# A four-layer graph network on one core: window sums carried by TensorE, VectorE's side work placed behind the messages, operands moved to PSUM

## The chip, the cores and the metric

The kernel runs on one core of a Trainium2 chip. The time is the device time of one execution in microseconds (us); before the change the median of three runs is 5459.54 us (5449.31 to 5473.62). The core has five engines with queues of their own, each in order: TensorE (PE in the profile; its weight loads are PEld), VectorE (DVE), ScalarE (ACT), GpSimd (POOL) and SyncE (SP). Here GpSimd does nothing but issue indirect DMAs, which gather or scatter one row of memory for each of 128 partitions, and SyncE issues the plain DMAs.

## The reference

Four layers update 6250 nodes of 160 numbers (64 scalars and 32 vectors of 3) over 100000 edges that are sorted by their target `dst`. Each layer does this, with its own weights and small differences:

```python
h = relu(layernorm(x))                    # nodes
f = h @ W_lin                             # node rows, "table" in the kernel
w = act(edge_features @ W_fc1) @ W_fc2    # weights of every edge
m = tensor_product(f[src], edge_attr, w)  # 384 numbers an edge (480 in layer 2)
agg = segment_sum(m, dst, N)
x = x + mix(agg @ W_out, h @ W_skip)
```

Layers 0, 1 and 3 gather by `src` and sum by `dst`. Layer 2 takes rows by `dst` and sums by `src`, by which the edges are not sorted.

## The kernel before

Edges are cut into 784 tiles of 128, and 14 tiles (`WT`) make a window; there are 56 windows. The edges of a window hit fewer than 128 nodes, since they are sorted. The tiles of a window's two halves alternate, and each half's targets fit in 64 nodes. Two windows make a unit `u`, and four tiles make a group `g`, so a layer has 196 groups. There is a second program for irregular inputs, which isn't taken here.

`edges(li)` (L1205 on) does layers 0, 1 and 3. For each group:

- `gather` (L1277): four indirect DMAs on GpSimd bring the rows `f[src]` of 128 edges each into `ge`. It is called six groups ahead, and there are eight `ge` buffers.
- `hidden` (L1266 or L1260, L1269) and `edge_weights` (L1300 or L1293, L1304, L1306): TensorE computes the edge weights, ScalarE brings them out of PSUM, partly scaled by an edge number, to `ws`.
- `messages` (L1313 to L1338): seven VectorE instructions. `oh` (L1319) is a one-hot of each edge's target among 64 nodes, from `iota` and the targets' places `loc`, both in SBUF. `pr`, `dot` and four parts of `msg` are products of `ge`, `ws` and edge numbers. The edge numbers were copied (L1313) for each unit into a PSUM tile, `yls`.
- TensorE adds `oh` times `msg` to `pg` in PSUM (L1394), 64 rows a half window. At a window's end ScalarE copies `pg` to `acc` (L1397).

Then `nodes` works on a window's 128 rows of `acc` as a Python generator, two steps of it a group. `turn` (L1346) is a matrix that puts the rows of both halves in order. In `nodes_out` four matmuls by `turn` make `pt_out` (L1062), ScalarE copies it to `at` (L1069), TensorE makes `po` (L1080, L1082), and VectorE adds to the node rows (L1095, L1096 and on). Then `nodes_in` makes the next layer's table: norm (L991 to L888), `hn` (L999), transposes (L1009, L1010), `pa` (L1022), `tb` (L1031 or L1033), and a DMA to memory. The next layer's first gather waits for all of it. A target on the border of two windows has part of its sum in each. Column 0 of `at` is the part that a window hands on, and VectorE adds it to column 1 of the next window's `at` (L1073).

In layers 0 and 1 another generator, `positions` (`self.sort`), sorts the edges by `src` for layer 2. For each of 53 buckets of 120 nodes and one more, VectorE makes `hit` (L1166), a running sum over 784 columns (the scan, L1168, from bfloat16 `hit` and `zeros_b` in SBUF), and two products or sums of 784 columns (L1171, L1172). One step is taken every third group.

Layer 2 has two stages. In `messages2` TensorE selects target rows out of `tb` (the window's 128 table rows) by a one-hot `oh` that VectorE makes of the window's targets (L1447: 1792 columns, from `dt`, a broadcast of the targets' numbers, L1445). `pe` (L1479) holds the selected rows, `pw` (L1468) the edge weights, VectorE makes `row` (L1497 to L1506), and GpSimd scatters each edge's 390 numbers to its sorted place (L1509). There are five `row` buffers. `sums2` then reads them back in order (L1601 to L1624) with plain DMAs.

The order of each engine's instructions is set when the program is built: a scheduler places the instructions of all these generators by its own estimate of times and priorities, so that node steps and sort steps stand between the messages of a group where it thinks they fit.

Of the kernel before, what the change touches and what calls it, by code (L numbers as in the profile page):

```python
# [689 lines left out]
class Fast:  # L690
# [16 lines left out]
    def prologue(self):  # L707
# [343 lines left out]
    def nodes_out(self, li, xt, sk, acc, turn, carry, w, wk, pp):  # L1051
# [5 lines left out]
        for k in range(4):  # L1057
            rows, o = (96, 3 * MV) if k == 0 else (MV, (k - 1) * MV)
            if turn is None:
                nc.tensor.transpose(pt[:rows, k, :], acc[:, o : o + rows], self.ident[:n, :n])  # L1060
            else:
                nc.tensor.matmul(pt[:rows, k, :], lhsT=acc[:, o : o + rows], rhs=turn, start=True, stop=True)  # L1062
        yield
# [4 lines left out]
        else:  # L1068
            nc.scalar.copy(at, pt)  # L1069
        if turn is not None:  # L1070

            if carry[0] is not None:
                nc.vector.tensor_add(at[:, :, 1], at[:, :, 1], carry[0][:, :, 0])  # L1073
            carry[0] = at
        yield
# [66 lines left out]
    def positions(self, wk):  # L1142
# [21 lines left out]
        for b in range(BK + 1):  # L1164
            hit = wk.tile([P, TT], BF16, name="hit2", bufs=2)
            nc.vector.tensor_scalar(hit, self.src_b, float(b), None, op0=ALU.is_equal)  # L1166
            cum = wk.tile([P, TT], F32, name="cum", bufs=2)
            nc.vector.tensor_tensor_scan(cum, hit, self.zeros_b, self.off[:, b : b + 1], op0=ALU.add,  # L1168
                                         op1=ALU.add)
# [29 lines left out]

    def at(self, k, most=N):  # L1200

        return self.nc.values_load(self.first[0:1, 2 * k : 2 * k + 1], engines=[mybir.EngineType.SP], min_val=0, max_val=most,
                                   skip_runtime_bounds_check_because="a node's number")

    def edges(self, li):  # L1205
# [19 lines left out]

        yls = p_y.tile([P, 2, 3, 2 * WT], F32, name="yls")

# [81 lines left out]
        def messages(u, g):  # L1309
            n = width(u, g)  # L1310
            rt, yl = data[u][0], yls[:, u % 2]
            if g == 0:
                nc.vector.tensor_copy(yl, rt[:, :, 1:4].rearrange("p t c -> p c t"))  # L1313
            ws = wss.pop((u, g))[:, :n]
            ge = gath.pop((u, g))[:, :n]
            gs = slice(G * g, G * g + n)
            oh = wk.tile([P, G, HN], F32, name="oh", bufs=3)
            t0 = 2 * WT * u + G * g
# [6 lines left out]
            yv = yl[:, :, gs].rearrange("p c t -> p t c")  # L1325
            t1 = msg[:, :, AW : AW + 64]
# [10 lines left out]
            tt(mvec[:, :, :, 0:64], by3(t1, 64), yv[:, :, :, None].to_broadcast([P, n, 3, 64]), ALU.mult)  # L1337
            tt(mvec[:, :, :, 64:96], e1, by3(ws[:, :, 64:96], 32), ALU.mult)  # L1338
            return oh, msg

        carry = [None]

        def nodes(k, acc):
            xt, sk = xts.pop(k)
            turn = nk.tile([P, P], F32, name="turn")
# [36 lines left out]
        for i, (u, g) in enumerate(groups):  # L1382
            prepare(i + AHEAD)
            weights_of(i + 2)
            if i + 1 < len(groups):
                edge_weights(*groups[i + 1])
            oh, msg = messages(u, g)
            for k in range(width(u, g)):
# [6 lines left out]
                if end:  # L1395
                    acc = wk.tile([P, AW], F32, name="acc")
# [14 lines left out]
    def messages2(self):  # L1411
# [26 lines left out]
        def select(k):  # L1438

            n = min(WT, TT - WT * k) * P  # L1440
            at = self.at(k)
            tb = ld.tile([P, 160], F32, name="tb")
            nc.sync.dma_start(tb, self.table[2][ds(at, P), :])
# [3 lines left out]
            nc.vector.tensor_scalar(oh.rearrange("p t e -> p (t e)")[:, :n], dt[:, :n], self.plus_w[:, k : k + 1], None,  # L1447
                                    op0=ALU.is_equal)
            ohs[k] = tb, oh
# [22 lines left out]
        def messages(u, g):  # L1472
            n = width(u, g)
            t0 = 2 * WT * u + G * g
            ts = slice(t0, t0 + n)
            pe = p_e.tile([P, G, 256], F32, name="pe")
            for k in range(n):
                tb, oh = ohs[(t0 + k) // WT]
                nc.tensor.matmul(pe[:, k, :160], lhsT=oh[:, (t0 + k) % WT, :], rhs=tb, start=True, stop=True)  # L1479
            pw = pws.pop((u, g))[:, :n]  # L1480
            pe = pe[:, :n]
            row = wk.tile([P, G, RW], F32, name="row", bufs=5)[:, :n]
            ev = wk.tile([P, G, 224], F32, name="ev", bufs=3)[:, :n]
            nc.scalar.copy(ev[:, :, 0:160], pe[:, :, 0:160])
            nc.scalar.copy(ev[:, :, 160:224], pe[:, :, 64:128])
            nc.scalar.copy(row[:, :, 294:390], pe[:, :, 64:160])  # L1486
            nc.scalar.copy(row[:, :, 256:262], self.edge_in[:, ts, :])
# [165 lines left out]
def _layout(inputs):  # L1653
# [46 lines left out]
    a["dst_t"] = by_tile(i["dst"], 1 << 20).T  # L1700
    a["dst_w"] = by_tile(i["dst"], 1 << 20).reshape(NW, WT * P)
    rec0 = np.zeros((E, 8), np.float32)
# [58 lines left out]
```

## Time and profile before

| what | value |
|---|---|
| median of runs | 5459.54 us |
| profiled execution, and its span | 5448.67, 5446.9 us |
| busy: PE, DVE, POOL, ACT | 4624, 4218, 3346, 2087 us |
| granted TensorE clock, mean | 0.881 |
| prologue up to the first gather | 171.4 us |
| layer 0, first to last gather | 171.4 to 1265.3 |
| layer 1, first to last gather | 1323.7 to 2394.8 |
| layer 2, first to last scatter | 2454.7 to 3549.9 |
| layer 2, sums | 3549.9 to 4379.9 |
| layer 3, first to last gather | 4379.9 to 5419.7 |
| one gather, min / median / max | 941 / 946 / 4311 ns |

A line of the groups' part reads: source line, engine, operation, tile written <- tiles read, how many; then busy us and mean ns of one; then the engine's idle time just before them and what ended it. In an order of time the columns are start, duration, engine, line. Busy time of TensorE is latency: matmuls overlap each other, so it is not occupancy.

### The profile page before, as it was taken

The page shows a single profiled execution, that of the slowest core. Times are in us where ns is not written, and L with a number is a line of the kernel's source. Part 1 is how long each engine was busy: PE and PEld are TensorE (multiplying, and loading weights), DVE is VectorE, ACT ScalarE, POOL GpSimd, SP SyncE. Part 2 cuts the span into 40 slices and gives each one's busy share as a digit, 9 for nine tenths or more (in the row PEclk, how much of TensorE's full clock was granted, in tenths as well). Part 3 has the DMA queues.
Part 4 walks back from the last instruction along what each step waited for, and adds up shares of the span by engine and source line. Part 5 has one row for each costly group of instructions (what it writes and reads, how often), then busy time and mean ns, then how long its engine had stood idle before and what let it go on. Part 6 is the DMA issues. An engine that isn't in the chain of part 4 may idle for free.

```text
span 5446.9 us, 77043 instructions
## 1 busy us (share of the span) xinstructions
PE 4624.0 (85%) x22084; PEld 2866.7 (53%) x22084; DVE 4217.8 (77%) x11655; ACT 2087.1 (38%) x6858; POOL 3346.0 (61%) x3143
## 2 busy tenths in 40 slices
PE   6799999997999999976666666689999988888887
PEld 4455555554555555544444444478888844444443
DVE  6688889888878897867777777767777767777777
ACT  5344444443544444533333333312222243343433
POOL 0577777774777777747777777700000067777776
PEclk9899999998989898987787877799999978788887
DMA  3333333322333333336666666477777533333332
GB/s 95 105 97 88 91 87 90 88 75 73 98 94 94 90 95 93 90 101 239 215 219 215 222 218 223 166 283 237 238 235 237 164 87 80 82 81 82 83 79 57
DMA packets 371211, 733.89 MB, mean 135 GB/s; under 512 B 69677, under 2 KB 249098, under 8 KB 370650
## 3 DMA queue, kind: packets, MB, share of 16 engines
q1 hardware_dynamic: 207122, 379.11, 22.3%
q0 software_dynamic: 163072, 349.43, 22.0%
q8 instruction: 180, 2.95, 0.2%
q14 instruction: 253, 2.07, 0.1%
q10 hardware_dynamic: 584, 0.33, 0.0%
HBM read 519.59 MB, written 209.08 MB: 134 GB/s over the span
## 4 chain that ended last, share of the span: by engine, by line
PE 52%; DVE 16%; DMA 14%; POOL 6%; issue 5%; ACT 3%; SPq 0%; DVEq 0%; ACTq 0%; POOLq 0%
PE pg L1394 12%; PE pg L1613 7%; DMA rec<-row,edge_to 7%; PE pw L1300 7%; DMA ge<-table,rt 6%; PE pg L1611 5%; POOL ge L1277 5%; PE ph L1266 4%; PE pa L1022 3%; PE pt_out L1062 2%; PE po L1082 2%; POOL rec L1509 2%; PE ph L1455 2%; DVE msg L1337 2%; PE pw L1293 2%
## 5 line engine op out<-in xcount | busy, mean ns | idle before, releaser
L1277 POOL DMA_INDIRECT ge<-table,rt x2352 | 2489.1, 1058 | 1774.1 <-DMA skip<-sk 830.3
L1394 PE MATMUL pg<-msg,oh 128*64 128x384 f32 x4704 | 1061.4, 572 | 165.6 <-DVE msg L1338 139.7
L1509 POOL DMA_INDIRECT rec<-row,edge_to x784 | 856.1, 1092 | 299.0 <-issue 191.2
L1304 ACT ACTIVATE ws<-pw,rt 128x96 f32<-128x96 f32 x2352 | 695.8, 348 | 820.5 <-DVE msg L1338 298.6
L1300 PE MATMUL pw<-w_w2y,hh 100*128 100x192 f32 x3136 | 673.5, 353 | 10.6 <-ACT ws L1306 7.7
L1394 PEld LDWEIGHTS pg<-msg,oh 128*64 128x64 f32 x4704 | 305.9, 150 | 709.0 <-issue 252.5
L1300 PEld LDWEIGHTS pw<-w_w2y,hh 100*128 100x128 f32 x3136 | 534.9, 202 | 236.9 <-ACT ws L1306 138.6
L1337 DVE TENSOR_TENSOR msg<-msg,yls 128x768 f32<-128x768 f32 x588 | 555.7, 945 | 0.0
L1613 PE MATMUL pg<-msg,oh 128*120 128x288 f32 x1668 | 541.5, 406 | 0.0
L1330 DVE TENSOR_TENSOR pr<-ge,yls 128x384 f32<-128x384 f32 x588 | 320.2, 545 | 220.7 <-DMA ge<-table,rt 219.9
L1269 ACT ACTIVATE hh<-ph 100x1024 f32<-100x1024 f32 (+1 forms) x336 | 269.1, 801 | 463.7 <-PE pw L1293 206.2
L1479 PE MATMUL pe<-tb,oh 128*128 128x160 f32 x1568 | 348.4, 363 | 112.5 <-ACT row L1486 112.3
L1266 PE MATMUL ph<-ft,w_w1r 12*100 12x512 f32 (+1 forms) x784 | 382.3, 658 | 71.2 <-ACT hh L1269 57.0
L1611 PE MATMUL pg<-rt,oh 128*120 128x192 f32 x1668 | 410.0, 328 | 29.3 <-DMA rt<-rec 29.3
L1479 PEld LDWEIGHTS pe<-tb,oh 128*128 128x128 f32 x1568 | 277.6, 226 | 274.5 <-ACT row L1486 221.9
L1333 DVE TENSOR_TENSOR msg<-ws,ge 128x512 f32<-128x512 f32 x588 | 402.0, 684 | 0.0
L1306 ACT COPY ws<-pw 128x192 f32<-128x192 f32 x1176 | 388.5, 330 | 0.0
L1455 PE MATMUL ph<-ft,w_w1d 128*128 128x512 f32 x224 | 162.4, 819 | 263.2 <-ACT hh L1457 262.4
L1502 DVE TENSOR_TENSOR row<-pw,ev 128x512 f32<-128x512 f32 x196 | 135.2, 690 | 301.8 <-ACT row L1488 298.3
L1611 PEld LDWEIGHTS pg<-rt,oh 128*120 128x120 f32 x1668 | 298.0, 184 | 117.6 <-issue 30.7
L1331 DVE TENSOR_REDUCE dot<-pr 128x128 f32<-128x384 f32 x588 | 344.2, 585 | 0.1
L1338 DVE TENSOR_TENSOR msg<-ge,ws 128x384 f32<-128x384 f32 x588 | 324.4, 552 | 0.0
(486 smaller groups left out, 7327.6 us busy)
## 6 DMA issues: line engine op xcount, KB each, us to landing
rt<-rec SPq DMA_DIRECT2D x208, 780.0 KB
dt<-in_dst_w_dram SPq DMA_DIRECT2D x56, 896.0 KB
ge<-table,rt POOLq DMA_INDIRECT x2352
ft<-in_ft_dram SPq DMA_DIRECT2D x56, 512.0 KB
ft<-in_ft_dram SPq DMA_DIRECT2D x28, 896.0 KB
xt<-x SPq DMA_DIRECT2D x168, 82.0 KB
rec<-row,edge_to POOLq DMA_INDIRECT x784
rt<-in_rec_dram SPq DMA_DIRECT2D x84, 112.0 KB
```

What stands on the lines that cost most here:

```text
L1266: nc.tensor.matmul(ph[:, i], lhsT=w1[r : r + K, :], rhs=ft[r : r + K, 4 * P * (j // 2) :][:, : 4 * P], start=True, stop=True)
L1277: nc.gpsimd.indirect_dma_start(out=ge[:, k, :], out_offset=None, in_=self.table[li], in_offset=bass.IndirectOffsetOnAxis(ap=rt[:, G * g + ...
L1300: nc.tensor.matmul(pw[:, i, :192], lhsT=hh[:, k + i, :], rhs=w2, start=True, stop=True)
L1304: nc.scalar.activation(ws[:, k0 + i, 0:96], pw[:, i, 0:96], AF.Copy, scale=rt[:, G * g + k0 + i, 0:1])
L1306: nc.scalar.copy(ws[:, k0 : k0 + m, 96:192], pw[:, :m, 96:192])
L1333: tt(msg[:, :, AW - 64 : AW + 64].rearrange("p g (k u) -> p g k u", k=2), ws.rearrange("p g (k u) -> p g k u", k=2)[:, :, :, 0:64], e0[:, ...
L1337: tt(mvec[:, :, :, 0:64], by3(t1, 64), yv[:, :, :, None].to_broadcast([P, n, 3, 64]), ALU.mult)
L1394: nc.tensor.matmul(pg[half], lhsT=oh[:, k, :], rhs=msg[:, k, :AW], start=t % WT < 2, stop=t % WT >= WT - 2)
L1479: nc.tensor.matmul(pe[:, k, :160], lhsT=oh[:, (t0 + k) % WT, :], rhs=tb, start=True, stop=True)
L1509: d = nc.gpsimd.indirect_dma_start(out=self.rec2, out_offset=bass.IndirectOffsetOnAxis(ap=self.edge_to[:, t0 + k : t0 + k + 1], axis=0), i ...
L1611: nc.tensor.matmul(pg[:, 0:192], lhsT=oh[:, k, :], rhs=rt[:, k, 0:192], start=first, stop=end, skip_group_check=True)
L1613: nc.tensor.matmul(pg[:, 192:480], lhsT=oh[:, k, :], rhs=msg[:, k, :], start=False, stop=end, skip_group_check=True)
```

## The change

- **Carried sums.** VectorE's addition of the handed-on column (L1073) is gone. In its place, after each of the four matmuls of `pt_out`, a matmul of one column adds the previous window's `acc` times column 0 of its `turn` onto column 1 of `pt_out`. `acc` and `turn` have four buffers each.
- **Node steps and sorting.** The steps of `nodes` and of `self.sort` that a group takes are built under `tc.issue_after(last.ins)`: their VectorE instructions may not stand before the group's last message instruction.
- **Operands in PSUM.** `yls` becomes part of a tile `bank`, which also holds the targets' places of a unit (copied from `loc`) and one zero. `oh` reads the targets there, and the scan reads the zero there, as float32.
- **Row groups in layer 2.** The 64 target nodes of a half window take one half of the partitions: `tb` and `dt` are loaded by halves, `oh` has half as many columns, and the matmuls of `pe` take 64 rows each, alternating between the two row halves and writing to two PSUM banks. `plus_w` is made from `column` to suit.

```diff
@@ prologue
-        nc.vector.tensor_scalar(self.plus_w, pw[:, 0, :], iota_p, None, op0=ALU.add)
         column = pro.tile([P, NW], F32, name="column0")
         nc.vector.tensor_scalar(column, pw[:, 1, :], place, None, op0=ALU.add)
+        nc.vector.scalar_tensor_tensor(self.plus_w, column, -1.0, pw[:, 0, :], op0=ALU.add, op1=ALU.add)
@@ nodes_out
-            else:
-                nc.tensor.matmul(pt[:rows, k, :], lhsT=acc[:, o : o + rows], rhs=turn, start=True, stop=True)
+                continue
+            nc.tensor.matmul(pt[:rows, k, :], lhsT=acc[:, o : o + rows], rhs=turn, start=True, stop=carry[0] is None,
+                             skip_group_check=True)
+            if carry[0] is not None:
+                sums, turned = carry[0]
+                nc.tensor.matmul(pt[:rows, k, 1:2], lhsT=sums[:, o : o + rows], rhs=turned[:, 0:1], start=False,
+                                 stop=True, skip_group_check=True)
+        if turn is not None:
+            carry[0] = acc, turn
...
-        if turn is not None:
-            if carry[0] is not None:
-                nc.vector.tensor_add(at[:, :, 1], at[:, :, 1], carry[0][:, :, 0])
-            carry[0] = at
@@ positions
-            nc.vector.tensor_tensor_scan(cum, hit, self.zeros_b, self.off[:, b : b + 1], op0=ALU.add,
+            nc.vector.tensor_tensor_scan(cum, hit, self.zero.to_broadcast([P, TT]), self.off[:, b : b + 1], op0=ALU.add,
                                          op1=ALU.add)
@@ edges
-        yls = p_y.tile([P, 2, 3, 2 * WT], F32, name="yls")
+        bank = p_y.tile([P, 8 * 2 * WT + 1], F32, name="bank")
+        yls = bank[:, : 8 * 2 * WT].rearrange("p (u c t) -> p u c t", u=2, c=4)
+        self.zero = bank[:, 8 * 2 * WT :]
+        nc.vector.memset(self.zero, 0.0)
...
-                nc.vector.tensor_copy(yl, rt[:, :, 1:4].rearrange("p t c -> p c t"))
+                nc.vector.tensor_copy(yl[:, 0:3], rt[:, :, 1:4].rearrange("p t c -> p c t"))
+                nc.vector.tensor_copy(yl[:, 3], self.loc[:, 2 * WT * u : 2 * WT * u + 2 * WT])
...
             tt(oh[:, :n], self.iota[:, None, :HN].to_broadcast([P, n, HN]),
-               self.loc[:, t0 : t0 + n, None].to_broadcast([P, n, HN]), ALU.is_equal)
+               yl[:, 3, gs, None].to_broadcast([P, n, HN]), ALU.is_equal)
...
-            tt(mvec[:, :, :, 64:96], e1, by3(ws[:, :, 64:96], 32), ALU.mult)
-            return oh, msg
+            last = tt(mvec[:, :, :, 64:96], e1, by3(ws[:, :, 64:96], 32), ALU.mult)
+            return oh, msg, last
...
-            live = [n for n in live if not (next(n, True) or next(n, True))]
+            with tc.issue_after(last.ins):
+                live = [n for n in live if not (next(n, True) or next(n, True))]
             if li < 2 and i % 3 == 0:
-                next(self.sort, None)
+                with tc.issue_after(last.ins):
+                    next(self.sort, None)
@@ messages2
-            dt = ld.tile([P, WT * P], I32, name="dt", bufs=2)
-            nc.sync.dma_start(dt[:, :n], self.a["dst_w"][k : k + 1, :n].to_broadcast([P, n]))
-            oh = ld.tile([P, WT, P], F32, name="oh", bufs=3)
+            dt = ld.tile([P, WT // 2 * P], I32, name="dt", bufs=2)
+            for h in range(2):
+                rows = slice(HN * h, HN * h + HN)
+                nc.sync.dma_start(tb[rows], self.table[2][ds(self.at(k, half=h), HN), :])
+                nc.sync.dma_start(dt[rows], self.a["dst_w"][2 * k + h : 2 * k + h + 1, :].to_broadcast([HN, WT // 2 * P]))
+            oh = ld.tile([P, WT // 2, P], F32, name="oh", bufs=3)
...
-                nc.tensor.matmul(pe[:, k, :160], lhsT=oh[:, (t0 + k) % WT, :], rhs=tb, start=True, stop=True)
+                h, rows = k % 2, slice(HN * (k % 2), HN * (k % 2) + HN)
+                nc.tensor.matmul(pe[:, 2 * h + k // 2, :160], lhsT=oh[rows, (t0 + k) % WT // 2, :], rhs=tb[rows],
+                                 start=True, stop=True)
```

More of the change, by code (lines that the diff above doesn't have):

```diff
@@ L1198, in layers, with at @@
         es.close()
-    def at(self, k, most=N):
-        return self.nc.values_load(self.first[0:1, 2 * k : 2 * k + 1], engines=[mybir.EngineType.SP], min_val=0, max_val=most,
+    def at(self, k, most=N, half=0):
+        return self.nc.values_load(self.first[0:1, 2 * k + half : 2 * k + half + 1], engines=[mybir.EngineType.SP], min_val=0, max_val=most,
                                    skip_runtime_bounds_check_because="a node's number")
@@ L1317, in messages @@
             oh = wk.tile([P, G, HN], F32, name="oh", bufs=3)
-            t0 = 2 * WT * u + G * g
             tt(oh[:, :n], self.iota[:, None, :HN].to_broadcast([P, n, HN]),
-               self.loc[:, t0 : t0 + n, None].to_broadcast([P, n, HN]), ALU.is_equal)
+               yl[:, 3, gs, None].to_broadcast([P, n, HN]), ALU.is_equal)
             msg = wk.tile([P, G, AW + 64], F32, name="msg", bufs=3)[:, :n]
@@ L1324, in messages @@
             e1 = ge[:, :, 64:160].rearrange("p g (c u) -> p g c u", c=3)
-            yv = yl[:, :, gs].rearrange("p c t -> p t c")
+            yv = yl[:, 0:3, gs].rearrange("p c t -> p t c")
             t1 = msg[:, :, AW : AW + 64]
@@ L1344, in nodes @@
             xt, sk = xts.pop(k)
-            turn = nk.tile([P, P], F32, name="turn")
+            turn = nk.tile([P, P], F32, name="turn", bufs=4)
             nc.vector.tensor_scalar(turn, self.iota, self.column[:, k : k + 1], None, op0=ALU.is_equal)
@@ L1386, in edges @@
                 edge_weights(*groups[i + 1])
-            oh, msg = messages(u, g)
+            oh, msg, last = messages(u, g)
             for k in range(width(u, g)):
@@ L1395, in edges @@
                 if end:
-                    acc = wk.tile([P, AW], F32, name="acc")
+                    acc = wk.tile([P, AW], F32, name="acc", bufs=4)
                     nc.scalar.copy(acc, pg)
@@ L1438, in select @@
         def select(k):
-            n = min(WT, TT - WT * k) * P
-            at = self.at(k)
             tb = ld.tile([P, 160], F32, name="tb")
-            nc.sync.dma_start(tb, self.table[2][ds(at, P), :])
-            dt = ld.tile([P, WT * P], I32, name="dt", bufs=2)
-            nc.sync.dma_start(dt[:, :n], self.a["dst_w"][k : k + 1, :n].to_broadcast([P, n]))
-            oh = ld.tile([P, WT, P], F32, name="oh", bufs=3)
-            nc.vector.tensor_scalar(oh.rearrange("p t e -> p (t e)")[:, :n], dt[:, :n], self.plus_w[:, k : k + 1], None,
+            dt = ld.tile([P, WT // 2 * P], I32, name="dt", bufs=2)
[4 more added lines that the diff above has]
+            oh = ld.tile([P, WT // 2, P], F32, name="oh", bufs=3)
+            nc.vector.tensor_scalar(oh.rearrange("p t e -> p (t e)"), dt, self.plus_w[:, k : k + 1], None,
                                     op0=ALU.is_equal)
@@ L1478, in messages @@
                 tb, oh = ohs[(t0 + k) // WT]
-                nc.tensor.matmul(pe[:, k, :160], lhsT=oh[:, (t0 + k) % WT, :], rhs=tb, start=True, stop=True)
+                h, rows = k % 2, slice(HN * (k % 2), HN * (k % 2) + HN)
+                nc.tensor.matmul(pe[:, 2 * h + k // 2, :160], lhsT=oh[rows, (t0 + k) % WT // 2, :], rhs=tb[rows],
+                                 start=True, stop=True)
+            pe = pe.rearrange("p (h t) c -> p t h c", h=2)
+            pair = lambda v: v.rearrange("p (t h) c -> p t h c", h=2)
             pw = pws.pop((u, g))[:, :n]
-            pe = pe[:, :n]
             row = wk.tile([P, G, RW], F32, name="row", bufs=5)[:, :n]
             ev = wk.tile([P, G, 224], F32, name="ev", bufs=3)[:, :n]
-            nc.scalar.copy(ev[:, :, 0:160], pe[:, :, 0:160])
-            nc.scalar.copy(ev[:, :, 160:224], pe[:, :, 64:128])
-            nc.scalar.copy(row[:, :, 294:390], pe[:, :, 64:160])
+            nc.scalar.copy(pair(ev[:, :, 0:160]), pe[:, :, :, 0:160])
+            nc.scalar.copy(pair(ev[:, :, 160:224]), pe[:, :, :, 64:128])
+            nc.scalar.copy(pair(row[:, :, 294:390]), pe[:, :, :, 64:160])
             nc.scalar.copy(row[:, :, 256:262], self.edge_in[:, ts, :])
@@ L1700, in _layout @@
     a["dst_t"] = by_tile(i["dst"], 1 << 20).T
-    a["dst_w"] = by_tile(i["dst"], 1 << 20).reshape(NW, WT * P)
+    a["dst_w"] = np.append(i["dst"], np.full(TT * P - E, 1 << 20, np.int32)).reshape(2 * NW, WT // 2 * P)
     rec0 = np.zeros((E, 8), np.float32)
```

## The prediction

> **What bounds the kernel now.** All durations are from the one profiled execution: 5448.67 us, span 5446.9. The median of the runs shown is 5459.5, 10.9 above it. I read the page first: engine sums, then the two indirect-DMA groups.
>
> ```profile
> PE 4624.0 (85%) x22084; PEld 2866.7 (53%) x22084; DVE 4217.8 (77%) x11655; ACT 2087.1 (38%) x6858; POOL 3346.0 (61%) x3143
> ...
> L1277 POOL DMA_INDIRECT ge<-table,rt x2352 | 2489.1, 1058 | 1774.1 <-DMA skip<-sk 830.3 <-issue 581.9 <-DVE w_osr L898 170.0
> L1509 POOL DMA_INDIRECT rec<-row,edge_to x784 | 856.1, 1092 | 299.0 <-issue 191.2 <-ACT ev L1485 62.1 <-DVE row L1502 14.6
> ```
>
> By shares TensorE would be the bound and POOL third. So I cut the span by first and last indirect DMA of each stage: layer 0, the hand-over, layer 1, hand-over, layer 2's messages, layer 2's sums, layer 3, tail (columns: stretch, length, then busy of PE, PEld, DVE, ACT, POOL with counts).
>
> ```profile
> 171.40:1265.30 1093.90, 1038.02 (x4970) 597.03 (x4972) 950.12 (x2616) 512.46 (x1598) 855.33 (x784) 0.92 0.35 90
> 1265.30:1323.70 58.40, 42.16 (x188) 23.83 (x184) 55.32 (x131) 17.65 (x54) 0.03 (x1) 0.78 0.23 65
> 1323.70:2394.80 1071.10, 1006.08 (x4666) 552.99 (x4666) 888.94 (x2534) 506.00 (x1700) 832.48 (x784) 0.91 0.35 92
> 2454.70:3549.90 1095.20, 699.30 (x3302) 470.03 (x3302) 778.48 (x1610) 373.62 (x1077) 856.13 (x784) 0.79 0.61 214
> 3549.90:4379.90 830.00, 809.27 (x4292) 680.59 (x4292) 602.35 (x1795) 178.00 (x691) 0.00 (x0) 0.98 0.70 228
> 4379.90:5419.70 1039.80, 881.57 (x4223) 450.87 (x4222) 805.25 (x2362) 404.91 (x1452) 801.25 (x784) 0.83 0.32 81
> ```
>
> Four stages hold 784 indirect DMAs each. The view of the gather's own line (min/median/max ns; idle before it) shows what lies between them:
>
> ```profile
> L1277 POOL DMA_INDIRECT ge<-table,rt x2352: 941/946/4311, 171.4 to 5418.8; - x196
> ...
>   issue: 581.9, 1910
> ...
>   DMA ge<-table,rt: 31.7, 104
> ```
>
> Within a stage no gap before a gather exceeds 313 ns (median 305), whoever is named as its releaser: POOL never waits for a buffer. So **POOL paces all four stages**, at 946 + 305 = 1251 ns an issue, 981 us for 784. The rest of each gather stage (113, 90, 59 us) is gathers longer than 946. In the order of time one sees why (two places):
>
> ```profile
> 979.09 1.84 DVE L1168 TENSOR_TENSOR_SCAN cum<-hit,off,zeros_b 128x784 f32<-128x784 bf16 x1
> 979.56 2.12 POOL L1277 DMA_INDIRECT ge<-table,rt  x1 [0.30 <-issue]
> ...
> 4606.82 0.95 DVE L1337 TENSOR_TENSOR msg<-msg,yls 128x768 f32<-128x768 f32 x1
> 4607.07 0.95 POOL L1277 DMA_INDIRECT ge<-table,rt  x1 [0.30 <-DVE turns L1129]
> ```
>
> The first gather ends 0.75 us after the scan's end; the second, under a VectorE instruction with `yls` in PSUM, takes 0.95. I matched every long gather with the VectorE instruction that ended 820 ns (750 for scans) before its end. Lost: layer 0: scans L1168 27.1, L1333 17.0, L1319 15.9, L1338 14.9, L1171 and L1172 16.3, L1336 7.5; layer 1: 17.6, 31.2, 5.2, 22.0, 10.5, 3.6; layer 3: L1319 18.9, L1333 16.4, L1336 16.0, L1338 7.3. In layer 2's messages (971 ns undisturbed) L1447 costs 17.1, L1497 to L1501 69. Instructions reading PSUM (L1337, L1330, L1502, L1505, L1506) cost nothing anywhere.
>
> VectorE's waits in the middle of layer 0 (total us, times, longest):
>
> ```profile
> DVE xt L1041 <- ACT tb L1033: 50.1, 18, 6.4
> DVE at L1073 <- ACT at L1069: 40.3, 22, 3.3
> DVE xt L1095 <- PE po L1082: 20.1, 32, 1.4
> ```
>
> In layer 0 the messages lag their gathers by 20 to 27 us from the 80th group on, so there VectorE's chain runs at POOL's pace; in layers 1 and 3 the lag is mostly 2 to 10.
>
> **The change, part by part.**
>
> *One-hot's targets and scans' zero in PSUM.* Neither instruction has two SBUF tensors any more, like L1337. The 45 stretched scans give back 27.1 + 17.6, the one-hots 15.9 + 5.2 + 18.9: 84.7 us of POOL. The new copy of the targets (28 a layer, between 0.15 and L1313's 0.31 us; I take 0.2) adds 5.6 us of VectorE a layer. A scan with an f32 zero in PSUM is not in the trace: from 0.97 (L1171, same length) to twice 1.84; I take 1.84, since L1330 with PSUM (545 ns) runs like L1338 without (552). [...] The row says 384/415/451 ns (min/median/max) for L1319: VectorE never waits. [...]
>
> *Carried sums by TensorE.* 165 adds of 162 ns and their wait leave VectorE (40.3 in 960 us of layer 0, 84.5 in layer 1's middle, 51.8 in layer 3's); 55 x 4 x 2 passes x 3 layers = 1320 one-column matmuls with a 96-column load come in. Nearest row, eight of pt_out in the chain of waits:
>
> ```profile
> 1219.59 0.87 PE pt_out L1062 x8
> ```
>
> (0.87 - 0.27 for one) / 7 = 86 ns apart, with 128 columns moving; so 40 to 86 ns each, 53 to 113 us in all. [...] Cost taken: 0, hidden under the gathers; were PE the bound, it would be paid in full. The new matmuls read the window before's `acc` and `turn`, long written, so no wait is added; `po` loses its wait for VectorE.
>
> *Node steps and sorting behind the group's last message.* The order of VectorE's instructions stays nearly the same in the steady part. What moves: seven sort steps (scan, multiply, add) that stood after layer 0's last message go into layer 1's groups, and two at the start move in. Now 35.8 us lie between the last message (1287.9) and layer 1's first gather; six scans at 1.85, twelve L1171/L1172 at 0.97 and hits stand in it. Layer 1's own end, the same chain without sorting, takes 14.3 us from last message (2403.2) to last `tb`, and 5.4 + 0.8 for the landing and issue seen at 1317.5: 20.5. Gain 15. Later by that: seven multiply-add pairs now stretch layer 1's gathers, 16.3/29 each, 4 us.
>
> *Layer 2 by row groups.* L1447 halves, 1171 to about 600 ns, off POOL's pace except where it blocks: the loss falls with the square (chance of a hit times length), 17.1 to about 5, gain 12 (0 to 17). The half-length matmuls relieve a PE at 699 of 1095: 0. SP now issues four loads and two register reads a window instead of two and one, with POOL's scatters unaffected; `dt` moves a half of the bytes. At the stage's start the 8.8 us `dt` landing is in the chain: gain 4 (-4 to 10). `plus_w` moves behind `column` in the prologue and is first read at 2429: 0.
>
> **Sum.** Layer 0: POOL's side 1093.9 - 43 = 1051. VectorE's side: 1104 from first to last message, less the adds 9 and their waits 46 (40.3 scaled), plus 6: 1055. Equal paces hold each other up, so I take 40, not 49, and 15 for the hand-over: -55. Layer 1: -17.6 - 5.2 + 4 = -19. Messages: -12, start -4. Layer 3: -19. Given back: a gather freed from one instruction meets the next later. Even sampling of L1333, L1338, L1336 (196 x D^2 / 2.5 us) would cost 67 us a layer, counted are 57 and 40 in layers 1 and 3; I add 10 (0 to 37). Total -99: 5350 from the profiled execution, 5361 from the median; I forecast the middle, 5355 (and count the rivals from 5454).
>
> **Rivals.** (1) *Given back*: the remaining two-input instructions reach even sampling (+27 more), and layer 0's VectorE chain yields 20 less. For: hits of L1319 were 5 to 19 by phase alone. Against: layers 1 and 3 wait for gathers, which fixes phases. 5400. [...] (3) *TensorE becomes the bound* in the edge stages (slower): busy reads 1038 of 1094 in layer 0. If busy were occupancy, slack is 50 us a layer, and 440 additions at a load's 163 + 60 ns take 98: +48 x 3, with POOL's gain hidden behind it, less 31 for hand-over and layer 2: 5454 + 113 = about 5570. It decides above 50/440 = 114 ns an addition. Against: POOL would then show gaps, and there are none. (4) *More*: layer 0 follows fully and hits thin out: 5310.
>
> **Chances.** Forecast 0.58, (1) 0.20, (4) 0.08, (2) 0.07, (3) 0.07. Its own range is 5315 to 5395; 8 in 10 with (1) and the edge of (4): 5300 to 5425. Under 0.5% (27 us, about what measurement tells) of change: 0.06, mostly (2); slower 0.07; faster 0.87.
>
> **What would show it.** Gathers in layer 0 and 1 above 2 us gone with the scans; L1319's successor followed by no long gather; first to last gather 1050, 1052, 1030 us; messages' scatters 1083; first gather of layer 1 some 55 us earlier; no `at` wait on VectorE. Wrong if gaps above 0.4 us appear before gathers (VectorE or TensorE then paces), if the scan's row exceeds 2.5 us, or if L1333 and L1338 hit more often.

## The result, and the profile after

The changed kernel is **slower**: 5535.8 us median of four runs (5516.4 to 5554.6) against 5466.6 us of the kernel before on the same chip, a ratio of 1.013 (95% interval 1.009 to 1.018). Forecast were 5355 us and a range of 5300 to 5425. The profiled execution has a span of 5545.9 us. The page's engine line and the two groups of indirect DMAs:

```profile
PE 4680.0 (84%) x23404; PEld 2954.1 (53%) x23404; DVE 4174.0 (75%) x11577; ACT 2078.4 (37%) x6858; POOL 3190.1 (58%) x3143
...
L1283 POOL DMA_INDIRECT ge<-table,rt x2352 | 2370.9, 1008 | 2004.0 <-PE ph L1266 831.3
...
L1521 POOL DMA_INDIRECT rec<-row,edge_to x784 | 818.4, 1044 | 323.1 <-issue 187.0
```

One gather fell from 1058 to 1008 ns on average, a scatter from 1092 to 1044: 118 and 38 us of GpSimd's time are gone (the prediction had 84.7 for the gathers and 12 for the scatters). But GpSimd's idle time before gathers rose from 1774 to 2004. The same cut by stages as before (layer 0, hand-over, layer 1, layer 2's messages, its sums, layer 3; then busy time of PE, PEld, DVE, ACT, POOL, granted clock, DMA):

```profile
171.90:1350.30 1178.40, 1112.94 (x5312) 647.87 (x5313) 942.48 (x2566) 507.03 (x1575) 799.40 (x784) 0.89 0.32 84
1350.30:1423.50 73.20, 63.98 (x276) 43.64 (x276) 44.54 (x145) 23.98 (x74) 0.07 (x2) 0.71 0.16 45
1423.50:2524.80 1101.30, 1043.30 (x4961) 594.56 (x4959) 884.57 (x2475) 491.16 (x1653) 789.77 (x784) 0.90 0.34 90
2609.40:3666.30 1056.90, 592.81 (x3298) 401.07 (x3298) 753.08 (x1609) 364.80 (x1073) 818.40 (x784) 0.72 0.59 199
3666.30:4497.60 831.30, 809.53 (x4292) 680.45 (x4292) 600.90 (x1793) 176.34 (x691) 0.04 (x1) 0.98 0.70 228
4497.60:5517.80 1020.20, 885.35 (x4654) 479.32 (x4654) 797.57 (x2338) 405.87 (x1453) 781.61 (x784) 0.87 0.33 83
```

| stage | before | after | difference | forecast |
|---|---|---|---|---|
| layer 0 | 1093.9 | 1178.4 | +84.5 | -40 |
| hand-over to layer 1 | 58.4 | 73.2 | +14.8 | -15 |
| layer 1 | 1071.1 | 1101.3 | +30.2 | -19 |
| hand-over to layer 2 | 59.9 | 84.6 | +24.7 | -4 |
| layer 2's messages | 1095.2 | 1056.9 | -38.3 | -12 |
| layer 3 | 1039.8 | 1020.2 | -19.6 | -19 |

(With 2 to 3 us from prologue, sums and tail this is the whole difference of 99.0 between the two profiled executions; the forecast column leaves out its +10 for what is given back.) The loss is in layers 0 and 1 and behind them, and there GpSimd now waits. The gather's own line, which had no gap above 0.313 us inside a stage before:

```profile
L1283 POOL DMA_INDIRECT ge<-table,rt x2352: 940/946/3178, 171.9 to 5516.8; - x196
...
  DVE bank L1320: 175.4, 17
  DVE bst L991: 150.3, 50
...
  DVE rstd L975: 32.6, 30
```

Adding up what goes beyond 0.313 us inside the stages gives 139.9 us in layer 0, 72.7 in layer 1, none in layer 3. In layer 0 the messages fall behind their gathers by 34 to 50 us (20 to 27 before) until all `ge` buffers are in use, and the gathers wait for messages.

What the prediction left out is the **chain of waits cut to the middle of layer 0** (500 to 1250 us). Its line of shares, before and after (the view ends its lines after 240 characters):

```profile
by line: PE pg L1394 25.3%; PE pw L1300 21.7%; PE ph L1266 13.7%; PE pa L1022 8.5%; PE pt_out L1062 5.1%; ACT hh L1269 3.5%; PE po L1082 2.9%; issue 1.9%; DVE msg L1337 1.9%; PE po L1080 1.4%; DVE msg L1333 1.2%; DVE cum L1168 1.2%; PE pt_i
```

```profile
by line: PE pg L1400 25.0%; PE pw L1306 21.2%; PE ph L1272 14.5%; PE pa L1022 7.8%; PE pt_out L1062 6.0%; ACT hh L1275 3.9%; PE po L1085 3.1%; issue 1.9%; PE pt_out L1067 1.8%; DVE msg L1343 1.5%; POOL ge L1283 1.3%; PE pt_in L1009 1.2%; DM
```

In the kernel **before**, nearly 80% of the chain is already TensorE. So I kept a ledger of TensorE for each stage: *idle* is time without any record of a matmul or a weight load; *lost* is the stage's length times one minus its granted clock; *covered* is the rest, taken as TensorE's work at full clock. By construction the three add up to the length (rounding can leave 1 us). The gathers' own time is their durations and 783 gaps of 0.305 us.

| run | layer 0: length = covered + idle + lost | gathers' own | layer 1: length = covered + idle + lost | gathers' own |
|---|---|---|---|---|
| before | 1094 = 951 + 56 + 87 | 1094 | 1071 = 908 + 65 + 98 | 1071 |
| after | 1178 = 985 + 65 + 128 | 1038 | 1101 = 928 + 58 + 115 | 1029 |

Before, TensorE was without work for 56 of layer 0's 1094 us, and the gathers never waited. Whether TensorE's chain had time to give away the ledger can't say by itself; the experiments have to.

### The profile page after: what moved, and what is told of

It reads as the page before. It is cut to its first block, busy times and chain, and to the rows that moved or that the text cites. A ratio compares the mean times of both kernels' runs of the same rounds, so it can differ in the third digit from the quotient of the medians.

```text
span 5545.9 us, 80013 instructions
## 1 busy us (share of the span) xinstructions
PE 4680.0 (84%) x23404; PEld 2954.1 (53%) x23404; DVE 4174.0 (75%) x11577; ACT 2078.4 (37%) x6858; POOL 3190.1 (58%) x3143
## 4 chain that ended last, share of the span: by engine, by line
PE 56%; DVE 13%; DMA 9%; POOL 8%; issue 6%; ACT 3%; SPq 0%; DVEq 0%; ACTq 0%; POOLq 0%
PE pg L1400 13%; PE pw L1306 8%; PE pg L1625 7%; DMA rec<-row,edge_to 5%; PE ph L1272 5%; PE pg L1623 5%; POOL rec L1521 5%; DMA ge<-table,rt 4%; PE pa L1022 4%; POOL ge L1283 4%; PE pt_out L1062 3%; PE po L1085 2%; PE pw L1299 2%; DVE msg L1343 2%; ACT hh L1275 2%
## 5 line engine op out<-in xcount | busy, mean ns | idle before, releaser
L1283 POOL DMA_INDIRECT ge<-table,rt x2352 | 2370.9, 1008 | 2004.0 <-PE ph L1266 831.3
L1400 PE MATMUL pg<-msg,oh 128*64 128x384 f32 x4704 | 1073.4, 578 | 125.9 <-DVE msg L1344 107.2
L1521 POOL DMA_INDIRECT rec<-row,edge_to x784 | 818.4, 1044 | 323.1 <-issue 187.0
L1306 PE MATMUL pw<-w_w2y,hh 100*128 100x192 f32 x3136 | 690.5, 360 | 16.0 <-ACT ws L1312 13.1
L1343 DVE TENSOR_TENSOR msg<-msg,bank 128x768 f32<-128x768 f32 x588 | 557.2, 948 | 0.0
L1272 PE MATMUL ph<-ft,w_w1r 12*100 12x512 f32 (+1 forms) x784 | 411.8, 666 | 82.6 <-ACT hh L1275 68.2
L1489 PE MATMUL pe<-tb,oh 64*128 64x160 f32 x1568 | 272.3, 407 | 225.0 <-ACT row L1498 222.0
L1336 DVE TENSOR_TENSOR pr<-ge,bank 128x384 f32<-128x384 f32 x588 | 321.2, 546 | 132.2 <-DMA ge<-table,rt 131.5
L1489 PEld LDWEIGHTS pe<-tb,oh 64*128 64x128 f32 x1568 | 205.8, 253 | 376.4 <-ACT row L1498 366.3
L1463 PE MATMUL ph<-ft,w_w1d 128*128 128x512 f32 x224 | 174.4, 876 | 208.1 <-ACT hh L1465 207.4
```

The source lines that it names most:

```text
L1272: nc.tensor.matmul(ph[:, i], lhsT=w1[r : r + K, :], rhs=ft[r : r + K, 4 * P * (j // 2) :][:, : 4 * P], start=True, stop=True)
L1283: nc.gpsimd.indirect_dma_start(out=ge[:, k, :], out_offset=None, in_=self.table[li], in_offset=bass.IndirectOffsetOnAxis(ap=rt[:, G * g + ...
L1306: nc.tensor.matmul(pw[:, i, :192], lhsT=hh[:, k + i, :], rhs=w2, start=True, stop=True)
L1400: nc.tensor.matmul(pg[half], lhsT=oh[:, k, :], rhs=msg[:, k, :AW], start=t % WT < 2, stop=t % WT >= WT - 2)
L1489: nc.tensor.matmul(pe[:, 2 * h + k // 2, :160], lhsT=oh[rows, (t0 + k) % WT // 2, :], rhs=tb[rows], start=True, stop=True)
L1521: d = nc.gpsimd.indirect_dma_start(out=self.rec2, out_offset=bass.IndirectOffsetOnAxis(ap=self.edge_to[:, t0 + k : t0 + k + 1], axis=0), i ...
```

## The experiments

Theories. **A**: TensorE paces layers 0 and 1, and the carried sums lengthen its queue. **B**: the steps held behind the last message make VectorE wait. When e1 and e3 had fitted neither, more came: **C**, TensorE paces layer 0, so that freed gathers gain nothing there; **D**, the one-hot waits for the copy of its targets; **E**, the operands in PSUM gave the scheduler other estimates, hence another order, and that costs TensorE; **F**, the operands or the copy of the targets themselves slow the chain. Ratios are to the kernel before, on the same chip; cuts by stage are from one profiled execution each.

### Parts undone, from the changed kernel

**e1**: carried sums back on VectorE.

```diff
-            if carry[0] is not None:
-                sums, turned = carry[0]
-                nc.tensor.matmul(pt[:rows, k, 1:2], lhsT=sums[:, o : o + rows], rhs=turned[:, 0:1], ...
...
+        if turn is not None:
+            if carry[0] is not None:
+                nc.vector.tensor_add(at[:, :, 1], at[:, :, 1], carry[0][:, :, 0])
+            carry[0] = at
```

> From the changed kernel (5536), only the carried sums go back to VectorE (the addition onto at; no one-column matmuls). Theory A (TensorE additions: 440 a layer lengthen TensorE's in-order queue, VectorE waits for po behind them): layers 0 and 1 come back to about 1050 and 1052 from first to last gather, total about 5380. Theory B (order: node steps held behind the last message make VectorE wait for po): layers stay near 1178 and 1100, total 5510 to 5540, and the waits of xt for po stay near 96 us in 500 to 1250.

**e2**: free order (both `with tc.issue_after(last.ins):` dropped); **e4**: only the one around the node steps dropped.

> From the changed kernel, only the rule that node and sort steps stand behind the group's last message is dropped. Theory A: still slow, 5500 to 5540, layer 0 above 1140. Theory B: 5380 to 5420, layer 0 near 1060, waits of xt for po back to 20 us; the hand-over before layer 1 grows by some 15.

> From the changed kernel, node steps are free again, sort steps still stand behind the last message. Theory A: 5500 to 5540. Theory B by node steps: 5380 to 5420, like the run with both free; by sort steps: near 5536.

**e3**: e1 and e2 together.

> Carried sums on VectorE and free order: what is left are the operands in PSUM and the row groups of layer 2. Both theories: 5365 to 5400 (5466 less some 85 in the gathers and messages, a part given back). If the operands or the row groups were themselves the loss: 5466 or more, with layer 0 above 1094.

Measured: e1 5482.3 (ratio 1.0027, 1.0007 to 1.0046); e2 5537.2 (1.0120, 1.008 to 1.016); e4 5546.0 (1.0144, 1.011 to 1.017); e3 5475.7 (1.0020, 1.0002 to 1.0037). Theory B falls: dropping the order changes nothing (5537 against 5536, and 5476 against 5482). The carried sums cost 54 us by the medians, 90 between the two profiled executions (that of e1 was one of its faster): 34 in layer 0, 26 in layer 1, 17 and 8 in the hand-overs behind them, 1 in layer 3. In the ledger, layer 0's covered time is 985, 986 and 985 with them (after, e2, e4), 951 in each of before, e1 and e3; layer 1's is 928 to 930 and 901 to 909. No run puts the carried sums alone into the kernel before. But e1 and e3 are **not faster than before**, against both theories. Layers 0 and 1 of e1:

```profile
172.00:1316.10 1144.10, 1066.81 (x4910) 602.70 (x4912) 949.71 (x2618) 505.30 (x1579) 795.24 (x784) 0.90 0.33 86
1372.00:2447.70 1075.70, 1008.36 (x4574) 553.96 (x4576) 897.75 (x2542) 495.55 (x1671) 794.15 (x784) 0.90 0.35 92
```

Layer 0 is 50 us longer than before although its gathers take 60 us less (795 instead of 855). Covered time is the old 951; idle is 77 instead of 56, lost 116 instead of 87. Something lets TensorE idle more and run more at the lower clock (0.90 granted instead of 0.92). Layer 2's messages (1055.8) and layer 3 (1019.1) keep their gains.

### One part at a time, and the order held

Instruction by instruction, in e7 some 520 of TensorE's 11,212 matmuls and about 1,000 of VectorE's instructions stand elsewhere than in the kernel with the row groups alone, whose order on TensorE is that of before outside layer 2's messages. So the order can be made a factor of its own: **e9** takes the places of TensorE's, ScalarE's and VectorE's instructions in the row-groups kernel as a list, and ties each instruction behind the one ahead of it, without a wait.

```diff
+    def hold(self):
+        traced = list(self.nc.cur_bb.bb.instructions)
...
+            turn = [i for i in (mine[k + at[k]] for k in range(len(at))) if i.name not in self.loose]
+            for a, b in zip(turn, turn[1:]):
+                self.tc.add_manual_dep(b, a.name, mybir.DependencyInfo(mybir.DependencyClass.NoSync, ...
```

**e7**: e3 with the scans' zero back in SBUF (and `acc` and `turn` with their old buffers), the scheduler's own order; e9 is e7 with the order held, but for the new copies of the targets and the one-hots of each layer's first unit. **e10**: row groups, and the one-hot's targets in PSUM if `li == 3` alone.

> Row groups of layer 2 and the one-hot's targets in PSUM; TensorE's, ScalarE's and VectorE's instructions held to the order of the kernel before (VectorE's but for the one-hots of each layer's first unit). Theory E (the PSUM operand changed the scheduler's order, and by that TensorE's idle gaps and its clock): layer 0 1080 to 1100 and layer 1 1050 to 1071, total 1.0 to 1.5% below before. Theory F (the operand or its copy slows the chain whatever the order): layer 0 1130 to 1150, total within 0.4% of before.

> The same operands with the scheduler's own order. Theory E: layer 0 1120 to 1150, layer 1 1070 to 1080, total within 0.4% of before. Theory F: the same as with the order held, within 10 us.

> Row groups of layer 2, and the one-hot's targets in PSUM in layer 3 alone: layers 0 and 1 are those of the kernel before in operands and in order. Layer 0 1094, layer 1 1071, messages of layer 2 1057, layer 3 1020; total 0.9 to 1.1% below before.

Measured (before 5469.7): e9 **5399.4** (0.9865, 0.9835 to 0.9894), e7 5444.4 (0.9952, 0.9937 to 0.9966), e10 5423.8 (0.9924, 0.9908 to 0.9941), a little short of its 0.9 to 1.1%: its hand-over to layer 1 took 66.4 us instead of 58.4. Layers 0 and 1 of e9, then layer 0 of e7:

```profile
171.40:1263.60 1092.20, 1035.03 (x4908) 592.16 (x4910) 947.21 (x2617) 508.58 (x1579) 835.45 (x784) 0.91 0.32 90
1342.80:2397.90 1055.10, 995.47 (x4634) 548.96 (x4634) 887.61 (x2553) 504.81 (x1691) 816.56 (x784) 0.91 0.34 94
```

```profile
171.90:1303.50 1131.60, 1061.26 (x4910) 601.14 (x4912) 946.08 (x2618) 504.43 (x1579) 820.77 (x784) 0.91 0.31 87
```

Theory E holds for the one-hot: the same operands in the old order give layer 0 1092 instead of 1132, and 45 us over all. Three engines' orders were held at once, so which of them matters isn't separated. With the order held, TensorE's idle time in layer 0 is 57 (56 before); with the scheduler's it is 70, and half of the growth lies at `pg` behind `ph` (11.6 instead of 5.3 us), where TensorE reaches the sums before VectorE has the messages. Layer 1 of e7, expected at 1070 to 1080, took 1054 and lost nothing. Yet even in e9 layer 0 gains nothing from gathers that are 20 us shorter (18.0 us of waits appear before them), while layer 1 gains 16: GpSimd paces layer 1 (1055 us, and its gathers by themselves take 1055), TensorE's chain layer 0. In the old order both limits of layer 0 stood at one value, 1092 for that chain and 1094 for the gathers.

The scans' zero was never run with the order held. e3, which has it in PSUM, takes 31 us more than e7 by the medians (on two chips where the kernel before differs by 3), with layer 1 at 1076 instead of 1054. Whether order or operand does that stays open. e10 shows what layer 2's row groups and layer 3's one-hot are worth by themselves, 46 us.

Its hand-over to layer 1 keeps e9 from more: 79.2 us (58.4 before, 55.9 in e3). What lengthened it I didn't settle.

### TensorE's pace, from both sides

**e11**: the changed kernel with each matmul of the carried sums followed by one that adds zero (column 0 of `iota` is zero).

```diff
                 nc.tensor.matmul(pt[:rows, k, 1:2], lhsT=sums[:, o : o + rows], rhs=turned[:, 0:1], start=False,
-                                 stop=True, skip_group_check=True)
+                                 stop=False, skip_group_check=True)
+                nc.tensor.matmul(pt[:rows, k, 1:2], lhsT=sums[:, o : o + rows], rhs=self.iota[:, 0:1], start=False,
+                                 stop=True, skip_group_check=True)
```

**e12**: e9 with ScalarE's order free, where `ph` and `hh` of layers 0 and 1 are made a group at a time.

```diff
-                ph = p_h.tile([H, 2, 4, P], F32, name="ph")
                 for i in range(n):
...
+                    ph = p_h.tile([H, 4, P], F32, name="ph", bufs=2)
...
+                    hh = wk.tile([H, 4, P], F32, name="hh", bufs=4)
+                    nc.scalar.activation(hh, ph, AF.Silu)
```

> The changed kernel with every matmul of the carried sums followed by another that adds zero (660 more, in two passes each). If TensorE sets the pace of layers 0 and 1, its covered time at full clock grows there by another 15 to 35 (the first set: 953 to 987 and 901 to 928), the layers by 30 to 60 each with idle and clock, layer 3 by nothing: total 1.0 to 2.0% above the changed kernel's 5536. If the first set's cost was a wait for the previous window's sums and not TensorE's time: within 15 of it.

> The kernel with the order held, and ph and hh of layers 0 and 1 as one buffer a group, two of them, instead of one of two groups: the wait of ph (33 us of TensorE's 55 us of idle in layer 0) goes, ScalarE makes each half by itself (one activation of 1.04 becomes two of some 0.6, 98 times a layer). If TensorE paces layer 0: down from 1092 to the gathers' own 1075, layer 1 unchanged at 1055 since GpSimd paces it, total 5375 to 5390 where the kernel with the order held has 5399. If ScalarE's additional 16 us a layer cost more than that: 5400 to 5420.

The edit of e12 comes from TensorE's waits in layer 0 of the kernel before (us, times, longest), which its ledger calls idle:

```profile
PE ph L1266 <- ACT hh L1269: 37.7, 38, 1.2
```

One `ph` buffer of two groups had to be emptied by ScalarE before TensorE could go on. Measured (before 5466.7): e11 5668.6 (1.0347, 1.028 to 1.041), e12 **5349.5** (0.9784, 0.975 to 0.982). e11's layers 0, 1 and 3, and e12's layers 0 and 1:

```profile
171.50:1430.40 1258.90, 1192.46 (x5738) 718.37 (x5740) 942.54 (x2566) 506.69 (x1579) 799.03 (x784) 0.86 0.28 78
1499.10:2675.00 1175.90, 1118.74 (x5377) 661.38 (x5375) 884.53 (x2475) 490.45 (x1653) 785.51 (x784) 0.85 0.30 84
4641.10:5650.40 1009.30, 920.72 (x5058) 516.76 (x5058) 797.36 (x2335) 403.29 (x1452) 770.72 (x784) 0.87 0.31 84
```

```profile
171.60:1240.60 1069.00, 1024.11 (x5017) 585.65 (x5018) 968.95 (x2677) 523.98 (x1700) 830.45 (x784) 0.95 0.33 92
1297.30:2346.30 1049.00, 988.69 (x4656) 547.75 (x4658) 893.60 (x2561) 513.60 (x1780) 810.44 (x784) 0.93 0.34 94
```

| run | layer 0: length = covered + idle + lost | gathers' own |
|---|---|---|
| e1, carried sums on VectorE | 1144 = 951 + 77 + 116 | 1034 |
| after | 1178 = 985 + 65 + 128 | 1038 |
| e11, carried sums twice | 1259 = 1015 + 66 + 177 | 1038 |
| e7, one-hot in PSUM | 1132 = 959 + 70 + 102 | 1060 |
| e9, the order held | 1092 = 940 + 57 + 96 | 1074 |
| e12, `ph` split | 1069 = 966 + 45 + 58 | 1069 |

The second set costs 80 us in layer 0 and 75 in layer 1, and nothing in layer 3 (1009 against 1020, and the gathers by themselves take 1010), where TensorE has slack: theory A is right. It is more than expected (30 to 60), since the clock took the greater part: of the 80, 30 are covered time and 49 lost. And with the wait for `hh` down from 38.1 us in e9 to 8.4, layer 0 falls to exactly what its gathers take by themselves; now GpSimd paces it. e12 is faster than both kernels, by 2.2% and 3.4%, and beats its 5375 to 5390. Of its 52 us under e9 between the profiled executions 23 are layer 0, 22 the hand-over behind it, 6 layer 1. It differs from e9 in two things: e9 with only ScalarE's order free was not run, so what that gave, in the hand-over above all, is not shown.

### Runs on two other chips

The first runs of single parts fell on two chips where the kernel before takes 6868 and 6614 us. In every trace kept from there ScalarE stops for some 1100 to 1600 us in sum; nothing in the trace releases it ("remote"; the view of ScalarE's waits of the row-groups kernel on one of them):

```profile
ACT acc L1395 <- remote: 243.1, 49, 8.4
ACT row L1490 <- remote: 213.4, 32, 14.6
ACT hh L1268 <- remote: 151.9, 25, 16.9
```

In all other traces this is zero. On the first of the slow ones: e5 (row groups alone), e6 (and the scans' zero), e7, and e8 (e3 with the targets copied at the fourth group of the unit before):

> The kernel before with only the row groups of layer 2. Messages of layer 2 near 1057 (the changed kernel had 1056.9, before 1095.2), all else as before: layer 0 1094, layer 1 1071, layer 3 1040. Total 5425 to 5435. If the row groups cost something elsewhere (hand-over before layer 2, 59.9 before, 84.6 changed), the hand-over would be above 65 and the total 5440 or more.

> Row groups and the scans' zero in PSUM; one-hot targets stay in SBUF. Theory C (TensorE paces layer 0, so a POOL freed of 27 us of scans gains nothing there): layer 0 1085 to 1100, layer 1 1055 to 1071, total 5405 to 5435. Theory D (what slows layer 0 is the new order behind the one-hot's wait for the copy of its targets): the same, since that copy is not here. If the scan's operand itself slowed layer 0: 1120 or more.

> Row groups and the one-hot's targets in PSUM; scans' zero stays in SBUF. Theory D (the copy of the targets at a unit's first group holds up oh, pg and TensorE's queue): layer 0 1130 to 1150 as with both operands, layer 1 about 1075, layer 3 about 1020, total 5465 to 5485. If the one-hot's operand were harmless: layer 0 1080 to 1100 and total 5400 to 5420.

> Both operands in PSUM and row groups, carried sums on VectorE, free order; the edge numbers and targets of a unit are copied at the fourth group of the unit before instead of at its own first group. Theory D: layer 0 back to 1060 to 1095, layer 1 near 1052, layer 3 near 1020, total 5350 to 5410. If the late copy was not the cause: layer 0 stays at 1130 to 1150, total 5465 to 5485.

Measured: 0.9990 (0.9965 to 1.0015), 1.0031, 1.0187 and 1.0381. On the second, e9, e7, e5 and e11 gave 1.0278, 1.0302, 1.0019 and 1.1125; they had been expected so:

> Row groups of layer 2 and the one-hot's targets in PSUM; TensorE's and ScalarE's instructions, and VectorE's but for a unit or so at each layer's start, are held to the order that they had in the kernel before. Theory E (the PSUM operand changed the scheduler's order, and by that TensorE's idle gaps and its clock): layer 0 1085 to 1100 and layer 1 1050 to 1070, as before or a little less; total 5385 to 5410 where before is 5467. Theory F (the operand or the copy of the targets slows VectorE or TensorE whatever the order): layer 0 1130 to 1150, total 5460 to 5480.

> The same operands with the scheduler's own order, on the same chip as the run with the order held. Theory E: layer 0 1125 to 1150, total 5455 to 5480. Theory F: the same as with the order held, within 10.

> The kernel before with only the row groups of layer 2, whose order on TensorE is that of before. Layer 0 1094, layer 1 1071, layer 3 1040 as before, messages of layer 2 near 1057, total 5425 to 5435 where before is 5467.

> The changed kernel with every matmul of the carried sums followed by another that adds zero (660 more, in two passes each). If TensorE sets the pace of layers 0 and 1, they grow by 30 to 45 each, as by the first set, and layer 3 by nothing: total 5600 to 5640 where the changed kernel has 5536. If the first set's cost was a wait for the previous window's sums and not TensorE's time: within 15 of 5536.

Here ScalarE's stops set the pace of the gather stages (layer 1 of e5 has 449 us of waits before gathers), so after the fact I drew nothing from them on the theories, though e9 had been expected to gain and lost 2.8%; e7, e9 and e11 were run once more on a chip without such stops. What is said above holds for such chips. That kernels with the targets' copy lose 2 to 4% on these chips stays unexplained.

## Why the prediction was wrong

By the medians 181 us lie between forecast and result. Of these 54 go with the carried sums (e1), 38 more with the scans' zero and the order rule (e7), 45 more with the order held (e9); the last 44 are what even e9 falls short, mainly in layer 0 and its hand-over.

- **"POOL paces all four stages" is the step that failed**, with "Cost taken: 0, hidden under the gathers". That GpSimd never waits shows that the chain behind it keeps up, with eight buffers of slack in between; it does not show that the chain has time left. In layer 0 TensorE's had none: in e9 the gathers need 1074 us and the stage still takes 1092. No run shows that cost of 0: taking the carried sums out again brings 54 us by the medians (e1). I had counted TensorE's work as some 3.3 of 5.6 us a group with node work, which was far too low; the items of that count (1.44 to 1.51 for each of the eight-packs of L1300 and L1394, about 0.5 for L1266) already make 3.45 without node work. The order of time in the kernel before, at a granted clock of 1.00, shows `ph` (L1266) at 1.1 and not 0.5:

```profile
701.15 1.49 PE L1300 MATMUL pw<-w_w2y,hh 100*128 100x192 f32 x8
702.58 1.10 PE L1266 MATMUL ph<-ft,w_w1r 12*100 12x512 f32 x2
703.60 1.51 PE L1394 MATMUL pg<-msg,oh 128*64 128x384 f32 x8
705.04 1.10 PE L1266 MATMUL ph<-ft,w_w1r 12*100 12x512 f32 x2
706.07 1.57 PE L1300 MATMUL pw<-w_w2y,hh 100*128 100x192 f32 x8
707.57 1.51 PE L1394 MATMUL pg<-msg,oh 128*64 128x384 f32 x8
709.01 1.57 PE L1300 MATMUL pw<-w_w2y,hh 100*128 100x192 f32 x8
```

  From the first start to the last lie two groups: 7.86 us, 3.93 each before node work. With it the ledger says 951 / 196 = 4.85 at full clock, and 5.58 with idle time and clock.
- **Rival 3 was the case that came** (given 0.07). Its decision point, 114 ns an addition, was wrong too. The first set costs 34 / 440 = 77 ns of covered time in layer 0, below that point and inside my 40 to 86, and it decides, since the chain had no slack and not 50 us. The whole price of the second set is 80 / 440 = 182 ns an addition, with the clock. No run shows the 60 ns that the rival adds to a load's 163.
- **The operands in PSUM: what they do for the gathers was right, the place of the gain wrong.** A scan with its zero in PSUM takes 1.84 us as taken, and gathers under it are no longer stretched:

```profile
1010.24 1.84 DVE L1171 TENSOR_TENSOR_SCAN cum<-hit,off,bank 128x784 f32<-128x784 bf16 x1
...
1010.58 0.95 POOL L1283 DMA_INDIRECT ge<-table,rt  x1 [0.30 <-DVE rstd L975]
```

  The excess of gathers over 946 ns fell from 113.7 to 57.8, 90.8 to 48.2 and 59.6 to 39.9 us in layers 0, 1 and 3; I had 43 less in layer 0. In the changed kernel only layer 3 could use it: 19.6 where 19 was forecast, and rival 1 (given back) did not come there.
- **"The order of VectorE's instructions stays nearly the same in the steady part"** left out what a moved operand does to the order, on TensorE and on VectorE. The order made for the one-hot's PSUM operand costs 45 us (e7 against e9). I had no term for it.
- **Carried sums, VectorE's side**: the wait for `at` is gone as forecast, but moved on. VectorE's waits in layer 0, 300 to 1345 us:

```profile
DVE xt L1098 <- PE po L1085: 128.2, 48, 6.7
DVE xt L1041 <- ACT tb L1033: 56.8, 24, 8.4
```

  The wait for `po` was 20.1. In e1, with the addition back on VectorE, it is 26.8 and that for `at` 80.0 (40.3 before): VectorE waits for TensorE's chain at whichever place comes first.
- **Node steps and sorting**: forecast -15 at the hand-over. e1 and e3, with and without the rule, have 55.8 and 55.9: it is worth nothing there. The hand-over's growth to 73.2 is the carried sums'.
- **Row groups**: -12 forecast, -38.3 measured. L1447's own stretches fell from 17.1 to 3.8, as forecast; the rest is that the messages' instructions (L1497 to L1501, now L1509 to L1513) hit 53 instead of 69 us, and that 9 us without a cause went. The size was off; why the messages' instructions hit less is not shown. The 8.8 us landing at the stage's start was no gain: hand-over 84.6 instead of 59.9 after, 58.6 in e10.

## What to carry to other kernels

An engine that never waits is not thereby the only bound: before moving work to another engine, cut the chain of waits to that stage, and add up covered time, idle time and lost clock of the engine that is to take it. Then test the slack with work that does nothing, as e11 does. When an operand moves, a scheduler may reorder queues far away; hold the order still and the two effects come apart. The largest gain over e9 came with neither: one buffer split in two, found in TensorE's list of waits (with ScalarE's order freed beside it).

## What the runs showed of the hardware

- **Short gaps often stand ahead of a drop of the clock, but are not all of it.** In layer 0 of the kernel before the longest gap in TensorE's work is 3.3 us, and TensorE ran at half clock in 31 stretches, 174 us in sum. 22 of them begin within 8 us after an idle gap above 0.9 us, though such times make up only 21% of the stage; most of these gaps are the 1.2 us waits for `hh`. e12 has 6 such gaps instead of 30, and 116 us at half clock. So gaps of some 1.2 us come ahead of most drops in the kernel before, and e12, with few of them left, loses 58 us to the clock instead of 87. That they cause the drops is likely, not shown: e12 keeps 23 drops, of which 2 follow such a gap, and the second set of additions (e11) raised the time at half clock from 256 to 355 us with idle time at 66 instead of 65. What else lowers the clock there no run isolates.
- **A one-column f32 matmul is not cheap.** The load of 96 columns takes as long as that of a full `pt_out` (minimum 161 and 159 ns, median 163 and 165), though one column moves instead of 128:

```profile
L1062 PEld LDWEIGHTS pt_out<-turn,acc x1344: 159/165/285, 207.7 to 5529.9; 128*96 128x96 f32 x192
...
L1067 PEld LDWEIGHTS pt_out<-turn,acc x1320: 161/163/283, 227.4 to 5530.3; 128*96 128x96 f32 x189
L1067 PE MATMUL pt_out<-turn,acc x1320: 165/217/299, 227.5 to 5530.4; 128*96 128x1 f32 x189
```

- **VectorE's one-hot takes the same time with either operand.** It took 384/415/451 ns (min, median, max) with its targets in SBUF, and with them in PSUM:

```profile
L1325 DVE TENSOR_TENSOR oh<-iota,bank x588: 381/414/434, 171.6 to 5519.0; 128x256 f32<-128x256 f32 x196
```

  Only GpSimd's gathers gained from the move: in layer 3, which has no scans, the 784 of them took 781.6 us instead of 801.3. That the one-hot doesn't wait, as the prediction read from its row, held.
- **Chips differ.** The kernel before took 5467 and 5470 us on two chips, 6614 and 6868 on two others; in the traces from these ScalarE stops, for causes that no record names.
